# More scan buffers, paid for with weights that are loaded when needed: a bidirectional state-space layer and a soft mixture of experts on one Trainium2 core

## The chip, the cores and the metric

The program runs on one core of one Trainium2 chip. A core has five engines that run side by side, each through its own instructions in a fixed order: TensorE (PE in the profile, its weight loads PEld), VectorE (DVE), ScalarE (ACT), GpSimd (POOL) and SyncE (SP), which here only issues DMA transfers. They wait for each other through semaphores. Working data lie in SBUF (128 partitions), matmul results in PSUM.

The metric is the device time of one execution in microseconds. Before the change its median was 5327.67 us over three runs (5324.82 to 5328.87).

## What is computed

The input is x, 16 sequences of 512 positions with 256 numbers each. The first layer is a state-space layer that runs in both directions, with a residual and a layer norm; the second is a soft mixture of 16 experts with 64 slots each, again with a residual and a layer norm.

```python
xr = x @ in_proj_w.T
xf, res = jnp.split(xr, [D_INNER], axis=-1)              # 512 channels each
xf = silu(causal_dw_conv(xf, conv_w, conv_b))
y = ssm(xf, res, ...)                                    # forward
xb = silu(causal_dw_conv(xf, conv_b_w, conv_b_b))
y = y + ssm(xb, res, ..., reverse=True)                  # backward
x = layernorm(x + y @ out_proj_w.T)

def ssm(x, res, x_proj_w, dt_proj_w, dt_proj_b, A_log, D, reverse=False):
    A = -jnp.exp(A_log)
    delta, B, C = jnp.split(x @ x_proj_w.T, [DT_RANK, DT_RANK + D_STATE], axis=-1)
    delta = softplus(delta @ dt_proj_w.T + dt_proj_b)    # the step sizes, dt
    y = selective_scan(x, delta, A, B, C, D, reverse=reverse)
    return y * silu(res)
...
logits = jnp.einsum('bnd,esd->bnes', layernorm(x), se)
dispatch = softmax(logits, axis=1)
combine = softmax(logits.reshape(b, n, -1), axis=-1)
slots = jnp.einsum('bnd,bnes->besd', layernorm(x), dispatch)
eout = ((gelu(slots @ Wg + bg) * (slots @ Wu + bu)) @ Wd + bd)   # per expert
out = layernorm(x + jnp.einsum('bns,bso->bno', combine, eout))
```

For each of 16 states and 512 channels the selective scan carries a value along the 512 positions: it is multiplied by exp(dt*A) at each step and dt*u*B is added. The result is gated with a factor close to 1 or to 0 (from the reference's small constant in a division), multiplied by C and summed over the states.

## The kernel before

**The scan loop.** `scan_part(b, r, p, ...)` handles batch b, direction r (0 forward, 1 backward) and a pair p of the four 128-channel chunks. It takes the 16 states two at a time, and each pair of states for one chunk is an item: 8 pairs of states x 2 chunks x 2 pairs of chunks x 2 directions x 16 batches are 1024 items. An item goes through the engines like this:

- SP loads B and C of two states, spread over the partitions, into `bs` (L431) and `cs` (L432), three buffers each.
- POOL multiplies du = dt*u by bs into `db` (L442): this is dt*u*B, in three buffers.
- ACT makes the decays exp(dt*A) into a PSUM tile `h` (L459, three buffers) and the gating factor `th` (L461, three).
- VectorE scans, h from decays and db (L465 forward, L467 backward), twice, and writes the gated states `hg` (L470), twice; hg has four buffers.
- POOL multiplies hg by cs in place (L471).
- TensorE adds hg, turned, onto the accumulator `acc` in PSUM (L386), eight pieces of 128 x 128. `add_up(2)` puts an item's add-up behind the work of the two items that follow it. Only then is the item's hg buffer free.

For a few states (four per direction for the first three batches, two later) the product with B goes over TensorE and a matrix with B on its diagonal (`hd`, L420, from `dg` and `duT`); such an item has only half a db tile.

**Side work.** Three queues of generators run beside the items, some pieces after each: `prep` (what the next scan needs), `front` (`finish` and `dispatch` of the batch before) and `back` (experts and combine). `HOLD` in them means that a PSUM bank is held until the next item, `BANKS = 3`. The experts of a pair of batches run beside the odd batches from the third on, the combine of both after them.

- `prep_pair` makes dt for two chunks: a matmul of the step-size weights `dtT` (17 rows, the last one the bias) with `xd` into `pz` (L320), softplus on ACT, a scan for rr on VectorE (L346), and du on POOL (L348). `dtT_f` and `dtT_b` were loaded once, in `steps`.
- `finish` turns the gated sum y over TensorE (`pyt`), copies it out (`yt`, L645), multiplies it by the output weights `outT` (`po`, L651), adds x, normalises, and makes `x2T`, which `dispatch` multiplies by the slots (`pl`, L710). `outT` was loaded once, in `constants`, and halved there by VectorE.
- `weights` makes the combine's softmax per 128 positions; `load_x2` loads a piece of x2T back into `cx2` (L917), which the matmuls `cl` (L933) read. The load of the next piece is issued right after the matmuls of the present one.

**Buffers and order.** A tag's tiles share a number of buffers, `bufs`; a tile that is written into a buffer waits until everything that read the last one is done. The language's scheduler orders each engine's instructions by the program's order, the free buffers and its own idea of their durations; `late` keeps an instruction in the program's order. SP issues in one order: a load that waits for its buffer holds all loads behind it.

The lines that hold the buffer counts and the order of an item's add-up:

```python
p4 = scan_room.enter_context(tc.tile_pool(name="m_scan", bufs=3))
...
db = p4.tile([P, 2, L], F32, tag="db", name=f"db_{q}_{c}")
...
hg = p4.tile([P, 2, L], F32, tag="hg", name=f"hg_{q}_{c}", bufs=4)
...
evict()
...
beside_scan()
...
add_up(2)
```

Of the kernel before, what the change touches and what calls it, by code (L numbers as in the profile page):

```python
# [17 lines left out]
P = 128  # L18
# [37 lines left out]
def seq_layers(tc, ident, neghalf, a, out):  # L56
# [22 lines left out]
    with ExitStack() as ctx:  # L79
# [76 lines left out]
            late(nc.vector.tensor_scalar(w["xT"][:, :, XC:XW], w["xT"][:, :, XC:XW], 0.5, None, ALU.mult))  # L156

        def steps(w, s, m):
            w["dtT"] = const.tile([DTR + 1, DI], F32, name=f"dtT_{s}")
            nc.sync.dma_start(w["dtT"][:DTR, :], a[f"dt_proj{m}T"])  # L160
            nc.sync.dma_start(w["dtT"][DTR : DTR + 1, :], a[f"dt_proj{m}_b"].unsqueeze(0))
            w["A"] = const.tile([P, ND, NS], F32, name=f"A_{s}")
            nc.sync.dma_start(w["A"], a[f"A{m}_log"].rearrange("(c p) n -> p c n", p=P))
            d = channels(a[f"D{m}"], f"D_{s}")
            w["diagD"] = const.tile([P, ND, P], F32, name=f"diagD_{s}")
            for c in range(ND):
                late(nc.vector.tensor_scalar(w["diagD"][:, c, :], ident, d[:, c : c + 1], None, ALU.mult))
# [7 lines left out]
        def constants():  # L175
            blanks(1)
            steps(side[0], "f", "")
            projections(side[1], "b", "_b")
            steps(side[1], "b", "_b")
            outT = const.tile([P, ND, DM], F32, name="outT")  # L180
            nc.sync.dma_start(outT, a["out_projT"].rearrange("(c p) o -> p c o", p=P))
            late(nc.vector.tensor_scalar(outT, outT, 0.5, None, ALU.mult))
            return outT

        projections(side[0], "f", "")
        blank = p2.tile([P, 4 * DM], F32, tag="W", name="blank", bufs=3)
# [125 lines left out]
        def prep_pair(b, r, p, v):  # L312

            w = side[r]
            yield GAP + 2
            pzs = []
            for c in (2 * p, 2 * p + 1):
                q = f"{b}_{r}_{c}"
                pz = bank(f"pz_{q}")
                nc.tensor.matmul(  # L320
                    pz, w["dtT"][:, c * P : (c + 1) * P], v["xd"][: DTR + 1, :], start=True, stop=True
                )
                pzs.append((c, q, pz))
            yield HOLD
            dts = {}
            for c, q, pz in pzs:
                dts[c] = dt = p4.tile([P, L], F32, tag="dt", name=f"dt_{q}", bufs=4)
                if len(dts) == 1:
                    act = nc.scalar.activation(dt, pz, AF.Softplus)
                    late(act)  # L330
                else:
                    with tc.high_priority():
                        nc.scalar.activation(dt, pz, AF.Softplus)
            yield HOLD
            for c, q, pz in pzs:
                dt = dts[c]

                rr = p4.tile([P, L], F32, tag="rr", name=f"rr_{q}", bufs=4)
                if r == 0:
                    edge, o, i = slice(L - 1, L), rr[:, 0 : L - 1][:, ::-1], slice(1, L)  # L340
                    ins = [t[:, i][:, ::-1] for t in (dt, pz)]
                else:
                    edge, o, i = slice(0, 1), rr[:, 1:L], slice(0, L - 1)
                    ins = [t[:, i] for t in (dt, pz)]
                nc.gpsimd.memset(rr[:, edge], 0.0)
                late(nc.vector.tensor_tensor_scan(o, ins[0], ins[1], 0.0, ALU.add, ALU.max))  # L346
                du = p4.tile([P, L], F32, tag="du", name=f"du_{q}", bufs=4)
                nc.gpsimd.tensor_tensor(du, dt, v["u"][:, c, :], ALU.mult)  # L348
                v[c] = [dt, rr, du]
# [57 lines left out]
        def scan_part(b, r, p, v, accs, done, then):  # L407
# [17 lines left out]
            for n in range(0, NS, 2):  # L425
                q = f"{b}_{r}_{p}_{n}"
                k = 1 if n + 1 in ds else 2

                bs = p4.tile([P, 2, L], F32, tag="bs", name=f"bs_{q}")
                cs = p4.tile([P, 2, L], F32, tag="cs", name=f"cs_{q}")  # L430
                nc.sync.dma_start(bs[:, :k, :], v["bc"][0, n : n + k, :].unsqueeze(0).to_broadcast([P, k, L]))  # L431
                nc.sync.dma_start(cs, v["bc"][1, n : n + 2, :].unsqueeze(0).to_broadcast([P, 2, L]))  # L432
                if n + 3 in ds:
                    dg = p4.tile([P, L], F32, tag="dg", name=f"dg_{q}", bufs=1)
                    nc.sync.dma_start(
                        dg.rearrange("p (l s) -> p l s", l=NL),
                        diag_dram[r, ds.index(n + 3), :, : P * P].rearrange("l (p s) -> p l s", p=P),
                    )
                for c in chunks:
                    dt, rr, du = v[c][:3]  # L440
                    db = p4.tile([P, 2, L], F32, tag="db", name=f"db_{q}_{c}")
                    nc.gpsimd.tensor_tensor(  # L442
                        db[:, :k, :], du.unsqueeze(1).to_broadcast([P, k, L]), bs[:, :k, :], ALU.mult
                    )
                    hg = p4.tile([P, 2, L], F32, tag="hg", name=f"hg_{q}_{c}", bufs=4)
                    hs = {}
                    for j in range(2):
                        if j < k:
                            dec = h = ps_h.tile([P, L], F32, tag="h", name=f"h_{q}_{c}_{j}")
                            hs[j] = (h, dec, db[:, j, :])  # L450
                        else:
                            h = made.pop((n + j, c))
                            dec = p4.tile([P, L], F32, tag="dec", name=f"dec_{q}_{c}", bufs=2)
                            hs[j] = (h, dec, h)

                    ths = {}
                    for j in range(2) if k == 2 else (1, 0):
                        s = slice(n + j, n + j + 1)
                        nc.scalar.activation(hs[j][1], dt, AF.Exp, scale=w["A"][:, c, s])  # L459
                        ths[j] = p4.tile([P, L], F32, tag="th", name=f"th_{q}_{c}_{j}")  # L460
                        nc.scalar.activation(ths[j], rr, AF.Tanh, bias=LN_1E12 / 2, scale=w["Ah"][:, c, s])  # L461
                    for j in range(2):
                        (h, dec, add), th = hs[j], ths[j]
                        if r == 0:
                            nc.vector.tensor_tensor_scan(h, dec, add, 0.0, ALU.mult, ALU.add)  # L465
                        else:
                            nc.vector.tensor_tensor_scan(  # L467
                                h[:, ::-1], dec[:, ::-1], add[:, ::-1], 0.0, ALU.mult, ALU.add
                            )
                        nc.vector.scalar_tensor_tensor(hg[:, j, :], th, 1.0, h, ALU.add, ALU.mult)  # L470
                    nc.gpsimd.tensor_tensor(hg, hg, cs, ALU.mult)  # L471
                    pending.append(
                        (r == n == 0, n == 0, r == 1 and n == NS - 2, c, hg, accs, w, v["u"], f"acc_{q}_{c}", done)
                    )
                    evict()

                    nxt_n = n if c == chunks[0] else n + 2
                    if nxt_n + 1 in ds:
                        for x in sides:
                            x.take_up()  # L480
                        by_diagonal(nxt_n + 1, chunks[1] if c == chunks[0] else chunks[0])
                    beside_scan()
                    if k == 1:
                        diags.pop(0)
                    add_up(2)
# [145 lines left out]
        def finish(b, y):  # L631

            xt = load_x(b)
            for h in range(NL // 2):
                yts = []
                for lc in (2 * h, 2 * h + 1):
                    yield 1
                    pt = bank(f"pyt_{b}_{lc}")
                    for c in range(ND):
                        nc.tensor.transpose(  # L640
                            pt[:, c * P : (c + 1) * P], y[:, c, lc * P : (lc + 1) * P], ident
                        )
                    yield HOLD
                    yt = p2.tile([P, L], F32, tag="fr", name=f"yt_{b}_{lc}")
                    late(nc.scalar.copy(yt, pt))  # L645
                    yts.append(yt)
                yield GAP + 1
                po = bank(f"po_{b}_{h}")
# [264 lines left out]
            expert_done.add(g)  # L913

        def load_x2(b, lc):
            t = p2.tile([P, NM, P], F32, tag="cx2", name=f"cx2_{b}_{lc}")
            nc.sync.dma_start(t, x2_dram[b, :, :, lc * P : (lc + 1) * P].rearrange("k p l -> p k l"))  # L917
            return t

# [119 lines left out]
        fwd = {}  # L1039
        prep.add(1, prep_forward(0, 0, ND, fwd))  # L1040
        prep.drain()
        outT = constants()
        prep.add(1, prep_pair(0, 0, 0, fwd))
        prep.drain()
        for w, s in zip(side, "fb"):
# [101 lines left out]
```

## Time and profile before

| what | us |
|---|---|
| median of three runs | 5327.67 |
| the profiled execution, its own time | 5322.25 |
| its span | 5320.5 |
| busy: POOL, VectorE, TensorE, ScalarE | 4681.6, 4560.6, 4310.4, 4104.9 |
| start of the last multiply of a gated state by cs (L471) | 5077.7 |
| L471 on POOL, one (median) | 2.362 |
| L442 on POOL, one of 128 x 1024 (median) | 2.357 |
| a scan (L465, L467) and a gated state (L470), one | 1.219, 0.679 |
| an add-up (L386), one of its eight pieces (median) | 0.273 |

In the profile a group's line gives the engine, the operation, the tile written and those read, the number of instructions, their busy time, the mean of one in ns, and after the second bar the idle time of the engine just before them with what ended most of it. A row of the waits says who waited for whom: the total in us, how often, and the longest. In a row of the timeline the first number is the start, the second the duration, and the square bracket the idle time of the engine before it. The slices cut the span into 40 equal parts of 133 us. Every engine's record can be put beside the item that it belongs to, since each engine's order is known; where a text says that the trace was paired item by item, this is what is meant.

### The profile page before, as it was taken

What the parts mean: (1) busy time and instruction counts of PE and PEld (TensorE: products, weight loads), DVE (VectorE), ACT (ScalarE), POOL (GpSimd) and SP (SyncE); (2) the same over time, 40 slices, a digit from 0 to 9 for tenths busy, and PEclk for the clock granted to TensorE, in tenths of its full rate; (3) what the DMA queues carried; (4) which work ended last, traced back from release to release, by engine and by line L of the source; (5) the groups of instructions that cost most, each with busy time, mean ns of one, the idle gap of its engine ahead of it and who ended that gap; (6) DMA issues with size and microseconds to landing.
All of it is one profiled execution on the core that took longest, in us unless ns stands there. A gap on an engine that the chain in (4) does not pass through costs nothing. (4 is left out here: it accounts for less than half of the span.)

```text
span 5320.5 us, 74550 instructions
## 1 busy us (share of the span) xinstructions
PE 4310.4 (81%) x24498; PEld 3411.1 (64%) x24498; DVE 4560.6 (86%) x6284; ACT 4104.9 (77%) x6573; POOL 4681.6 (88%) x2537
## 2 busy tenths in 40 slices
PE   5677776897778978788788878889787897878889
PEld 3556565676567756676666766667666676657667
DVE  7999999889998899888898888988898889987733
ACT  6777878887888877888887887888778887777644
POOL 6999999989999899999999989998999989988710
PEclk7778888998899989999899988899888998889999
DMA  5444444675446644576446754467544664447545
GB/s 141 137 129 152 126 142 131 211 234 152 146 146 224 222 144 143 171 226 206 132 140 198 236 169 151 134 210 230 157 151 144 217 227 149 144 153 230 168 135 168
DMA packets 614820, 907.82 MB, mean 171 GB/s; under 512 B 84606, under 2 KB 404734, under 8 KB 614432
## 3 DMA queue, kind: packets, MB, share of 16 engines
q1 hardware_dynamic: 532740, 859.35, 50.9%
q10 hardware_dynamic: 81692, 43.70, 3.1%
q8 instruction: 195, 3.19, 0.2%
q14 instruction: 193, 1.58, 0.1%
HBM read 840.34 MB, written 62.56 MB: 170 GB/s over the span
## 5 line engine op out<-in xcount | busy, mean ns | idle before, releaser
L471 POOL TENSOR_TENSOR hg<-hg,cs 128x1024 f32<-128x1024 f32 x1024 | 2416.9, 2364 | 125.0 <-DVE hg L470 108.0
L442 POOL TENSOR_TENSOR db<-du,bs 128x1024 f32<-128x1024 f32 (+1 forms) x1024 | 2087.7, 2042 | 227.8 <-DVE h L465 84.1
L470 DVE SCALAR_TENSOR_TENSOR hg<-th,h 128x512 f32<-128x512 f32 x1744 | 1156.8, 679 | 183.4 <-PE acc L386 105.9
L386 PE MATMUL acc<-ident,hg 128*128 128x128 f32 x8192 | 1163.6, 292 | 106.4 <-POOL hg L471 84.6
L386 PEld LDWEIGHTS acc<-ident,hg 128*128 128x128 f32 x8192 | 1034.4, 152 | 284.6 <-POOL hg L471 131.3
L467 DVE TENSOR_TENSOR_SCAN h<-h,db 128x512 f32<-128x512 f32 x872 | 1044.9, 1219 | 104.9 <-ACT h L459 92.6
L465 DVE TENSOR_TENSOR_SCAN h<-h,db 128x512 f32<-128x512 f32 x872 | 1044.1, 1219 | 44.5 <-ACT h L459 43.6
L461 ACT ACTIVATE th<-rr,Ah_f 128x512 f32<-128x512 f32 x1024 | 724.6, 714 | 200.9 <-DVE hg L470 198.1
L461 ACT ACTIVATE th<-rr,Ah_b 128x512 f32<-128x512 f32 x1024 | 721.3, 712 | 153.5 <-DVE hg L470 143.5
L459 ACT ACTIVATE h<-dt,A_f 128x512 f32<-128x512 f32 x872 | 591.4, 680 | 99.5 <-DVE hg L470 96.3
L459 ACT ACTIVATE h<-dt,A_b 128x512 f32<-128x512 f32 x872 | 592.3, 680 | 85.6 <-DVE hg L470 81.7
L420 PE MATMUL hd<-dg,duT 128*128 128x128 f32 x2432 | 375.7, 305 | 73.2 <-ACT duT L364 27.1
L420 PEld LDWEIGHTS hd<-dg,duT 128*128 128x128 f32 x2432 | 347.9, 220 | 84.5 <-ACT duT L364 29.5
L710 PE MATMUL pl<-x2T,seT 128*128 128x512 f32 x512 | 294.1, 704 | 78.4 <-DVE hg L470 37.4
L838 PE MATMUL peo<-Wd,ht 128*128 128x256 f32 x1024 | 258.1, 408 | 63.2 <-DVE rr L346 36.6
L869 PEld LDWEIGHTS pg<-st,Wg 128*128 128x128 f32 x2048 | 243.1, 195 | 94.1 <-issue 82.8
L811 PE MATMUL pu<-st,Wu 128*128 128x128 f32 x2048 | 255.6, 284 | 49.3 <-DMA Wu<-in_Wu_dram 27.0
L1015 PE MATMUL cpo<-ceo,ct 128*128 128x256 f32 x1024 | 256.0, 407 | 43.2 <-DVE rr L346 40.0
L811 PEld LDWEIGHTS pu<-st,Wu 128*128 128x128 f32 x2048 | 245.9, 199 | 60.6 <-DVE h L467 29.5
L838 PEld LDWEIGHTS peo<-Wd,ht 128*128 128x128 f32 x1024 | 205.5, 206 | 106.1 <-DVE rr L346 39.2
L869 PE MATMUL pg<-st,Wg 128*128 128x128 f32 x2048 | 265.0, 284 | 4.5 <-DMA st<-s_dram 3.4
L1015 PEld LDWEIGHTS cpo<-ceo,ct 128*128 128x128 f32 x1024 | 207.2, 207 | 87.2 <-DVE rr L346 42.7
(165 smaller groups left out, 6754.0 us busy)
## 6 DMA issues: line engine op xcount, KB each, us to landing
cs<-bc SPq DMA_DIRECT2D x512, 512.0 KB, 3.9
bs<-bc SPq DMA_DIRECT2D x360, 512.0 KB, 5.2
Wg<-in_Wg_dram SPq DMA_DIRECT2D x128, 512.0 KB, 5.7
Wu<-in_Wu_dram SPq DMA_DIRECT2D x128, 512.0 KB, 5.8
Wd<-in_Wd_dram SPq DMA_DIRECT2D x128, 512.0 KB, 5.5
dg<-diag_dram SPq DMA_DIRECT2D x152, 256.0 KB, 4.3
bs<-bc SPq DMA_DIRECT2D x152, 256.0 KB, 3.5
x<-in_x_dram SPq DMA_DIRECT2D x32, 512.0 KB, 6.5
```

What stands on the lines that cost most here:

```text
L386: ins = nc.tensor.matmul(accs[c][:, s], hc[:, j, s], ident, is_transpose=True, start=False, stop=(last and j == 1 and lc == NL - 1),)
L420: ins = nc.tensor.matmul(h[:, s], v[c][3][:, s], dg[:, s], start=True, stop=True)
L442: nc.gpsimd.tensor_tensor(db[:, :k, :], du.unsqueeze(1).to_broadcast([P, k, L]), bs[:, :k, :], ALU.mult)
L459: nc.scalar.activation(hs[j][1], dt, AF.Exp, scale=w["A"][:, c, s])
L461: nc.scalar.activation(ths[j], rr, AF.Tanh, bias=LN_1E12 / 2, scale=w["Ah"][:, c, s])
L465: nc.vector.tensor_tensor_scan(h, dec, add, 0.0, ALU.mult, ALU.add)
L467: nc.vector.tensor_tensor_scan(h[:, ::-1], dec[:, ::-1], add[:, ::-1], 0.0, ALU.mult, ALU.add)
L470: nc.vector.scalar_tensor_tensor(hg[:, j, :], th, 1.0, h, ALU.add, ALU.mult)
L471: nc.gpsimd.tensor_tensor(hg, hg, cs, ALU.mult)
L811: nc.tensor.matmul(pu[:, fc * P : (fc + 1) * P], got["Wu", e][:, k, fc * P : (fc + 1) * P], st[:, k, :, j * SL : (j + 1) * SL], start=(k = ...
L838: nc.tensor.matmul(po[:, j * DM : (j + 1) * DM], ht[:, fc, :], got["Wd", e0 + j][:, fc, :], start=(fc == 0), stop=(fc == NF - 1),)
L869: nc.tensor.matmul(pg[:, fc * P : (fc + 1) * P], got["Wg", e][:, k, fc * P : (fc + 1) * P], st[:, k, :, j * SL : (j + 1) * SL], start=(not ...
```

## The change

Two tags get one buffer more: hg five instead of four, db four instead of three. Room is made in three places. The step-size weights are no longer kept; each `prep_pair` loads the 256 columns that it needs, in two pieces, into one buffer. The output weights are no longer kept either; each `finish` loads them into the buffer of x2T, and the factor 0.5 moves from the weights to the copy of the turned y (a scaled activation in place of a copy). And cx2 has one buffer instead of two.

```diff
         def steps(w, s, m):
-            w["dtT"] = const.tile([DTR + 1, DI], F32, name=f"dtT_{s}")
-            nc.sync.dma_start(w["dtT"][:DTR, :], a[f"dt_proj{m}T"])
-            nc.sync.dma_start(w["dtT"][DTR : DTR + 1, :], a[f"dt_proj{m}_b"].unsqueeze(0))
+            w["dtT"] = [(slice(0, DTR), a[f"dt_proj{m}T"]), (slice(DTR, DTR + 1), a[f"dt_proj{m}_b"].unsqueeze(0))]
...
             steps(side[1], "b", "_b")
-            outT = const.tile([P, ND, DM], F32, name="outT")
-            nc.sync.dma_start(outT, a["out_projT"].rearrange("(c p) o -> p c o", p=P))
-            late(nc.vector.tensor_scalar(outT, outT, 0.5, None, ALU.mult))
-            return outT
...
         def prep_pair(b, r, p, v):
             w = side[r]
+            dtT = p1.tile([DTR + 1, 2 * P], F32, tag="dtT", name=f"dtT_{b}_{r}_{p}")
+            for rows, src in w["dtT"]:
+                nc.sync.dma_start(dtT[rows, :], src[:, 2 * p * P : 2 * (p + 1) * P])
             yield GAP + 2
...
-                    pz, w["dtT"][:, c * P : (c + 1) * P], v["xd"][: DTR + 1, :], start=True, stop=True
+                    pz, dtT[:, (c - 2 * p) * P : (c - 2 * p + 1) * P], v["xd"][: DTR + 1, :], start=True, stop=True
...
-                    db = p4.tile([P, 2, L], F32, tag="db", name=f"db_{q}_{c}")
+                    db = p4.tile([P, 2, L], F32, tag="db", name=f"db_{q}_{c}", bufs=4)
...
-                    hg = p4.tile([P, 2, L], F32, tag="hg", name=f"hg_{q}_{c}", bufs=4)
+                    hg = p4.tile([P, 2, L], F32, tag="hg", name=f"hg_{q}_{c}", bufs=5)
...
         def finish(b, y):
             xt = load_x(b)
+            outT = p1.tile([P, ND, DM], F32, tag="x2T", name=f"outT_{b}")
+            nc.sync.dma_start(outT, a["out_projT"].rearrange("(c p) o -> p c o", p=P))
...
-                    late(nc.scalar.copy(yt, pt))
+                    late(nc.scalar.activation(yt, pt, AF.Identity, scale=0.5))
...
         def load_x2(b, lc):
-            t = p2.tile([P, NM, P], F32, tag="cx2", name=f"cx2_{b}_{lc}")
+            t = p2.tile([P, NM, P], F32, tag="cx2", name=f"cx2_{b}_{lc}", bufs=1)
...
-        outT = constants()
+        constants()
```

## The prediction

> **What bounds the kernel now.** I read the busy shares first, then the slices, then the groups of the scan loop, then the waits.
>
> ```profile
> PE 4310.4 (81%) x24498; PEld 3411.1 (64%) x24498; DVE 4560.6 (86%) x6284; ACT 4104.9 (77%) x6573; POOL 4681.6 (88%) x2537
> ...
> POOL 6999999989999899999999989998999989988710
> ...
> L471 POOL TENSOR_TENSOR hg<-hg,cs 128x1024 f32<-128x1024 f32 x1024 | 2416.9, 2364 | 125.0 <-DVE hg L470 108.0
> L442 POOL TENSOR_TENSOR db<-du,bs 128x1024 f32<-128x1024 f32 (+1 forms) x1024 | 2087.7, 2042 | 227.8 <-DVE h L465 84.1
> L470 DVE SCALAR_TENSOR_TENSOR hg<-th,h 128x512 f32<-128x512 f32 x1744 | 1156.8, 679 | 183.4 <-PE acc L386 105.9
> ```
>
> POOL is the fullest engine, at nine tenths or more nearly everywhere until the scans end (last multiply by cs ends at 5080.1 us); the last 240 us hold almost no POOL work. Of 4788 us between 133 and 4921 us it works 4466 (the forty slices of the windows view, its first and last ones left out), so 322 us is the most that any smoother feed can give. An item (one pair of states for one chunk, 1024 of them) costs POOL 2.04 + 2.36 = 4.40 us, while the scans take about 4.9 us an item. The line L470 holds the wait that the fifth buffer is about: VectorE stands 105.9 us before writing a gated state because TensorE has not yet added up the one that held the buffer.
>
> ```profile
> DVE hg L470 <- PE acc L386: 105.9, 89, 4.8
> ...
> DVE h L467 <- POOL db L442: 11.5, 4, 3.2
> ```
>
> These are two rows of the waits of VectorE: total, times, longest. Waiting for dt*u*B costs it 11.5 us in all. One such stall, in the timeline near 2460 us:
>
> ```profile
> 2459.41 1.23 DVE L467 TENSOR_TENSOR_SCAN h<-h,db 128x512 f32<-128x512 f32 x1 [0.18 <-ACT h L459]
> 2463.01 1.28 DVE L470 SCALAR_TENSOR_TENSOR hg<-th,h 128x512 f32<-128x512 f32 x2 [2.37 <-PE acc L386]
> ...
> 2461.93 1.04 PE L386 MATMUL acc<-ident,hg 128*128 128x128 f32 x8
> ...
> 2464.43 2.37 POOL L471 TENSOR_TENSOR hg<-hg,cs 128x1024 f32<-128x1024 f32 x1 [2.61 <-DVE hg L470]
> ```
>
> TensorE did expert matmuls from 2455.96 and came to the add-up at 2461.93; VectorE lost 2.37 us and POOL, right after it, 2.61. So a late TensorE reaches the fullest engine through the four buffers.
>
> **Part 1, fifth hg buffer.** I paired the trace item by item. POOL's multiply of an item ends a median 9.0 us before the add-up of the same item ends (three quarters within 11.7, worst 24.4), but begins only 2.25 us after VectorE finished it. So buffers are held by TensorE's lag, not by POOL's. In the paired records 92 items have such a stall, 107.5 us, and 95.5 of these lie in stalls under 3 us. One buffer more is worth one item, 4.9 us; the two longest stalls are 4.79 and 4.13. So nearly all can go. How much reaches POOL: matching each stall with POOL's idle time for the same item gives 33.5 us, and with the next item's too 66.0. The same-item match misses idle that comes one step later, the other may count idle with another cause; I take the middle, 50 us. Both ends stay for the range, and so does all of it, 107.5.
>
> **Part 2, fourth db buffer.** Alone it gives nothing. In the built order POOL's multiplies by cs stood 4 db products behind (886 of 1024; now 5, 891 of 1024). Before, product i+3 waited for the scan of item i to free one of three buffers and came just ahead of multiply i, which needs item i as well. Now product i+4 waits for that same scan, and comes just ahead of the same multiply. POOL stays tied to the same event of VectorE; VectorE gets one product more in reserve, worth at most the 11.5 us above. I take 0 (bounds 0 and 11.5).
>
> The Trainium skill's "Perfetto Trace Analysis", section Identifying Performance Opportunities (Optimization Strategy), says that repeating gaps on the engine that should be full can mean too few buffers. Read so, POOL's 125.0 + 227.8 us before L471 and L442 would go, leaving about 4975 us; the pairing disagrees, since POOL then waits for the same item one instruction later.
>
> **Part 3, step-size weights.** 64 pairs now load two pieces each (16 and 1 rows of 256 numbers), 128 issues less four at the start. An issue costs SP 0.32 to 0.4 us (the rows of cs and cx), so some 45 us on a queue with 2126 issues that mostly waits. The single buffer makes the load wait for the previous pair's pz (L320). Behind it in SP's new order stand bs and cs loads. Putting the old trace's times of that pz against the release of the last cs ahead of it, SP is held at most 9.9 us in the running stage (43.8 once at the start, where nothing is ahead). But a cs lands at least 10.9 us, median 20.4, before its multiply, and a bs mostly 13 or more; the weights still land over 20 us before pz. The cover is those landings: 0. Were it gone, 64 holds of about 6 us would cost up to 384.
>
> **Part 4, output weights.** 16 loads of 512 KB, each into the buffer of x2T, after the last use of the previous one (L710). By the same pairing that use is at most 1.8 us later than SP's position, and po (L651) needs the tile 45 us or more later, against landings of 3.7 to 6.5 us. 8 MB more beside 908. The 0.5 moves from one VectorE instruction at the start into 64 evictions on ACT: 586 ns as COPY (L645), 680 to 770 as a scaled ACTIVATE (L727: 716; L691: 770): 64 x 0.10 to 0.19 = 6 to 12 us on an engine 77% busy. PE waits for yt in all some 33 us (15.4 + 13.6 + 2.4 + 1.6), so a few of them are on the path; I take 5 of 0 to 12.
>
> **Part 5, one cx buffer.** 60 loads of 128 KB wait for the cl matmuls just ahead (L933) instead of those one block back. The next use comes 7.7 us later at the closest (block 14, in the last 100 us) and mostly 12 to 25 later; landings take 2.5 to 5.4. Once, near 4970 us, SP is held 15.8 us with two cs behind it, less than the 20 us they usually have. I take 0; were all eight late ones 2 us short, 16.
>
> POOL and VectorE will overlap a little more. The multiplies by cs run 2332 to 2418 ns, whatever VectorE does beside them, so I cost that at 0; if every POOL product went from median 2362 to 2418, 2048 of them would add 115 us. The Trainium skill's "GPSIMD Engine Reference", section Key points, speaks against the change here: the two share their SBUF interfaces, and contend when a VectorE instruction has two inputs in SBUF. In the loop VectorE's second input is h in PSUM, and the narrow spread shows no such contention; by the rule the upper bound just named would be the thing to fear.
>
> **Sum.** 50 - 5 = 45 us off a span of 5320.5, so 5275.5. Around it lie 1.75 us (the profiled execution took 5322.25), and the median shown, 5327.67, is 5.4 above that: 5283.
>
> **Rivals.**
>
> *The gain stays off the path (no change).* VectorE also waits for ACT's decays (92.6 + 43.6 us), for th (39.4) and in its side work for TensorE (72.4 for pl, 56.7 for peo). And in the expert slices TensorE is all but full: 123.63 of 133 us between 1064 and 1197. A late add-up there is not jitter; one more buffer is used up once and the stalls return. For: by the pairing 96.8 of the 107.5 us lie in the odd batches from 3 on, where experts run, 9 to 10 in each such slice. Against: they come singly (batch 7, 2161 to 2494 us, has eleven, of 13.6 us together, mostly 20 us and more apart, each shorter than one item), and over that batch TensorE works 289.39 of 333 us. With 5 to 15 us passing and 5 lost: 5327, range 5317 to 5333.
>
> *TensorE is fed later (slower).* The built order puts VectorE's side work up to four instructions, a whole item, further behind the scans: ht by 1.18 places on average, eo 1.17, xf 1.27, x 1.78, nm 0.82, while TensorE's order stays. Summed over the groups (128 of ht, 128 of nm, 64 each of cnm, eo, xf, cx, 32 of x and of its moments) that is some 635 places, at 0.95 us (mean of 1.22 and 0.68) about 600 us of later feeding. It costs if those places aren't made up by VectorE no longer standing still: TensorE waits for the evictions, falls behind, and the add-ups with it, so that the fifth buffer fills too. It decides from where more than 50 of the 600 reach POOL. Following the waits back from the last multiply, TensorE holds 1268 of 5080 us of the chain, a quarter; a sixth of 600 less the 45 gained gives 5327.7 + 100 - 45 = 5383. For: in-order TensorE and three banks. Against: places aren't time; an order that puts a scan first also starts it sooner.
>
> *Everything passes (much faster).* All 107.5 with 0 lost: 5220.
>
> **How the numbers follow.** The forecast has 0.58 with its own range 5262 (66) to 5300 (33 less 5), everything passing 0.07, off the path 0.15, later feeding 0.20. Changes under 0.2%, 10.7 us, can't be told from none here. Faster by more than that: 0.65 (the forecast, everything passing); within: 0.15; slower: 0.20. The range 5225 to 5345 takes in the forecast with nearly all of its upper bound, the no-change case and the mild half of later feeding; what it leaves out is everything passing in full and the heavy half.
>
> **What will show it.** The row of VectorE's hg waiting for acc should fall from 105.9 under 40 us, POOL's idle before L471 and L442 from 353 to about 300, and the last multiply should end near 5035. Waits for db should stay near nothing, SP's holds unseen by POOL (bs and cs never named as releasers). Nearly all of it should come from the odd batches (about 332 us each now, with 29 us of POOL idle; the even ones take 312, with 13) and from the last. Wrong would be: TensorE's waits for ht, eo, rr or nm grown by as much as the acc wait fell, or acc still named for 80 us and more.

## The result, and the profile after

The changed kernel took 5368.91 us (median of four runs, 5361.69 to 5372.8), the kernel before in the same comparison 5327.72 us. The ratio is 1.0077, interval [1.0059, 1.0094]: 41 us slower, where 45 us faster had been forecast. The profiled execution took 5365.79 us, with a span of 5363.6.

First the busy shares and POOL's slices of the changed kernel, then the groups that answer to those of before; the lines of the file have moved by three, so L468, L439 and L467 are the old L471, L442 and L470.

```profile
PE 4329.2 (81%) x24498; PEld 3412.6 (64%) x24498; DVE 4541.6 (85%) x6283; ACT 4111.3 (77%) x6578; POOL 4681.7 (87%) x2537
...
POOL 6999999989999899898999889998999989988710
...
L468 POOL TENSOR_TENSOR hg<-hg,cs 128x1024 f32<-128x1024 f32 x1024 | 2422.6, 2369 | 103.8 <-DVE hg L467 60.1
L439 POOL TENSOR_TENSOR db<-du,bs 128x1024 f32<-128x1024 f32 (+1 forms) x1024 | 2092.5, 2047 | 284.5 <-DVE h L462 146.1
L467 DVE SCALAR_TENSOR_TENSOR hg<-th,h 128x512 f32<-128x512 f32 x1744 | 1155.6, 677 | 161.1 <-PE acc L383 74.2
```

POOL has the same work, 4681.7 us against 4681.6, and the others within 19 us of theirs. What grew is standing still. The wait that the fifth buffer was for fell, from 105.9 to 74.2 us, and POOL's wait for gated states from 108.0 to 60.1. But POOL's wait to write db, for a scan that is still to come, rose, and its idle time before both products went from 352.8 to 388.3 us (103.8 + 284.5). So the question is what held the scans. The waits of the changed kernel, ScalarE's rows first and then VectorE's (total, times, longest):

```profile
ACT x L622 <- POOL m_sh L617: 86.3, 16, 7.7
ACT cx L622 <- POOL c_sh L617: 79.6, 21, 6.3
...
DVE h L464 <- ACT h L456: 113.7, 54, 5.9
DVE hg L467 <- PE acc L383: 74.2, 44, 4.9
DVE cx L1025 <- PE cpo L1016: 73.2, 26, 4.9
```

The same places in the kernel before:

```profile
ACT cx L625 <- POOL c_sh L620: 64.8, 21, 7.0
...
ACT x L625 <- POOL m_sh L620: 42.6, 15, 6.2
...
DVE h L467 <- ACT h L459: 92.6, 95, 3.2
...
DVE cx L1024 <- PE cpo L1015: 31.0, 19, 4.3
```

The row of ACT x doubled. It belongs to the layer norm in `finish`: VectorE makes mean and variance (`m_mv`, L52), POOL four small instructions that end in the shift `m_sh` (L614 to L617), and ScalarE scales x by them (L622). VectorE's wait for decays has fewer and longer pieces: 54 of up to 5.9 us where there were 95 of up to 3.2.

To see where the time lies I paired both traces item by item and took each batch from its first scan to the next one's:

```
us per batch        even, 4 to 14 (mean of 6)    odd, 5 to 13 (mean of 5)
before              306.1                        328.9
change              314.8                        329.8
```

The even batches lost 8.7 us each, 52 in six; the odd ones are nearly as they were, batch 3 gained 4 us and batch 15 gained 10. In each of the six even batches ScalarE stands once before it scales x: 0.45 to 0.87 us before, 6.5 to 7.7 us in the change. One such place, batch 8, in the timeline of the changed kernel:

```profile
2585.54 0.18 DVE L52 BATCH_NORM_AGGREGATE m_mv<-m_st 128x2 f32<-128x6 f32 x1
2585.80 1.34 POOL L439 TENSOR_TENSOR db<-du,bs 128x512 f32<-128x512 f32 x1
2587.03 2.41 POOL L468 TENSOR_TENSOR hg<-hg,cs 128x1024 f32<-128x1024 f32 x1
2589.33 1.32 POOL L439 TENSOR_TENSOR db<-du,bs 128x512 f32<-128x512 f32 x1
2590.56 0.29 POOL L614 TENSOR_SCALAR m_rs<-m_mv 128x4 f32<-128x4 f32 x1
...
2584.01 1.05 ACT L964 COPY ct<-ctp 128x512 f32<-128x512 f32 x2
2592.76 0.60 ACT L622 ACTIVATE x<-x,m_sh,m_rs 128x256 f32<-128x256 f32 x1 [7.70 <-POOL m_sh L617]
2593.26 0.67 ACT L456 ACTIVATE h<-dt,A_b 128x512 f32<-128x512 f32 x1
2593.88 1.05 ACT L361 COPY duT<-pdu 128x512 f32<-128x512 f32 x2
2593.97 1.23 DVE L464 TENSOR_TENSOR_SCAN h<-h,db 128x512 f32<-128x512 f32 x1 [5.88 <-ACT h L456]
2594.50 6.53 PE L1016 MATMUL cpo<-ceo,ct 128*128 128x256 f32 x16 [6.24 <-ACT duT L361]
```

And in the kernel before:

```profile
2572.53 0.18 DVE L52 BATCH_NORM_AGGREGATE m_mv<-m_st 128x2 f32<-128x6 f32 x1
...
2576.28 0.22 POOL L617 TENSOR_SCALAR m_rs<-m_mv 128x4 f32<-128x4 f32 x1
...
2577.39 0.57 ACT L274 ACTIVATE res<-pres 128x512 f32<-128x512 f32 x1
2578.41 2.08 ACT L625 ACTIVATE x<-x,m_sh,m_rs 128x256 f32<-128x256 f32 x4 [0.45 <-POOL m_sh L620]
...
2574.61 3.62 PE L1015 MATMUL cpo<-ceo,ct 128*128 128x256 f32 x16
```

Read it from VectorE on. The statistics are ready at 2585.72, but POOL first does three products and comes to the factors at 2590.56, 4.8 us later (before: 3.6); making them takes 2.1 to 2.2 us in both kernels. ScalarE is in order; it reached the scaling at 2585.06, 0.7 us ahead of the statistics. In the kernel before it came at 2577.96, 5.3 us after them. So of the 7.25 us by which the stand grew, 5.9 are ScalarE's earlier arrival, the same in each of the six even batches, and 1.3 are POOL's. Until 2592.76 the decay for the next scan (L456) and the copy of du for the diagonal matmuls (`duT`, L361) stand behind the scaling. VectorE's scan waits 5.88 us for that decay, TensorE 6.24 us for that copy, and its next 16 matmuls take 6.53 us instead of 3.62.

The built order of the even batches explains why ScalarE meets the factors so early. Counted in items, VectorE's statistics come half an item later than before (in batch 4 beside item 273.0 instead of 272.5), the scaling on ScalarE half an item earlier (274.5 instead of 275.0, counted by its gating factors), and on POOL five products of du stand ahead of the factors beyond the multiplies by cs, instead of three. Nothing of that is in the diff: the scheduler places instructions by the free buffers, and their number changed.

### The profile page after: what moved, and what is told of

It reads as the page before. It is cut to its first block, busy times and chain, and to the rows that moved or that the text cites. A ratio compares the mean times of both kernels' runs of the same rounds, so it can differ in the third digit from the quotient of the medians.

```text
span 5363.6 us, 74655 instructions
## 1 busy us (share of the span) xinstructions
PE 4329.2 (81%) x24498; PEld 3412.6 (64%) x24498; DVE 4541.6 (85%) x6283; ACT 4111.3 (77%) x6578; POOL 4681.7 (87%) x2537
## 5 line engine op out<-in xcount | busy, mean ns | idle before, releaser
L468 POOL TENSOR_TENSOR hg<-hg,cs 128x1024 f32<-128x1024 f32 x1024 | 2422.6, 2369 | 103.8 <-DVE hg L467 60.1
L439 POOL TENSOR_TENSOR db<-du,bs 128x1024 f32<-128x1024 f32 (+1 forms) x1024 | 2092.5, 2047 | 284.5 <-DVE h L462 146.1
L467 DVE SCALAR_TENSOR_TENSOR hg<-th,h 128x512 f32<-128x512 f32 x1744 | 1155.6, 677 | 161.1 <-PE acc L383 74.2
L456 ACT ACTIVATE h<-dt,A_f 128x512 f32<-128x512 f32 x872 | 592.0, 681 | 115.3 <-DVE hg L467 112.0
L456 ACT ACTIVATE h<-dt,A_b 128x512 f32<-128x512 f32 x872 | 591.1, 679 | 69.4 <-DVE hg L467 67.2
L417 PEld LDWEIGHTS hd<-dg,duT 128*128 128x128 f32 x2432 | 337.0, 214 | 102.6 <-ACT duT L361 35.0
L1016 PE MATMUL cpo<-ceo,ct 128*128 128x256 f32 x1024 | 265.1, 418 | 78.1 <-DVE rr L343 38.6
L870 PEld LDWEIGHTS pg<-st,Wg 128*128 128x128 f32 x2048 | 257.8, 205 | 97.5 <-issue 80.1
L870 PE MATMUL pg<-st,Wg 128*128 128x128 f32 x2048 | 281.1, 295 | 5.6 <-DMA st<-s_dram 3.8
## 6 DMA issues: line engine op xcount, KB each, us to landing
dg<-diag_dram SPq DMA_DIRECT2D x152, 256.0 KB
bs<-bc SPq DMA_DIRECT2D x152, 256.0 KB
```

Of the source, the lines that this page charges most:

```text
L417: ins = nc.tensor.matmul(h[:, s], v[c][3][:, s], dg[:, s], start=True, stop=True)
L439: nc.gpsimd.tensor_tensor(db[:, :k, :], du.unsqueeze(1).to_broadcast([P, k, L]), bs[:, :k, :], ALU.mult)
L870: nc.tensor.matmul(pg[:, fc * P : (fc + 1) * P], got["Wg", e][:, k, fc * P : (fc + 1) * P], st[:, k, :, j * SL : (j + 1) * SL], start=(not ...
L1016: nc.tensor.matmul(po[:, :DM], cts[sc // 4][:, sc % 4 * P : (sc % 4 + 1) * P], eos[sc // 4][:, sc % 4, :], start=(sc == 0), stop=(sc == NS ...
```

## The experiments

Eleven kernels were run, one of them twice. Every ratio is to the kernel before, run beside them on the same chip; its medians there were 5327 to 5333 us.

**One part of the change at a time.** First hg five, db back at three:

```diff
-db = p4.tile([P, 2, L], F32, tag="db", name=f"db_{q}_{c}", bufs=4)
+db = p4.tile([P, 2, L], F32, tag="db", name=f"db_{q}_{c}", bufs=3)
```

> The change with db back at three buffers; hg keeps five, the loads stay as the change has them. Theory A (ScalarE stands before the layer norm's scaling, because GpSimd's factors come later while the scaling comes earlier on ScalarE): in the built order of the even batches from 4 on the statistics stay half an item later on VectorE and the scaling half an item earlier on ScalarE, but only one product of dt*u*B more stands ahead of the factors on GpSimd (4 instead of 3, the change has 5). The stand in even batches falls from 7.7 us to 5 or 6, and the time to 5345-5362 us. Theory B (TensorE is fed later throughout, by VectorE's side work behind the scans): the side work is as late as in the change, so 5360-5375. Theory C (the added loads hold SP and through it the scans): 5360-5375.

Measured 5377.95 us, 1.0089 [1.0075, 1.0102]: the whole loss without the fourth product, and above what any of the three theories had given. ScalarE's row is there in full (`ACT x` for `m_sh`: 85.5 us), and the even batches take 313.0 to 315.7 us.

Then db four, hg back at four:

```diff
-hg = p4.tile([P, 2, L], F32, tag="hg", name=f"hg_{q}_{c}", bufs=5)
+hg = p4.tile([P, 2, L], F32, tag="hg", name=f"hg_{q}_{c}", bufs=4)
```

> The change with hg back at four buffers; db keeps four, the loads stay. Theory A: statistics and scaling stand as before the change, one product more is ahead of the factors on GpSimd; the stand in even batches is 1.5 to 3.5 us (0.5 to 0.9 before, 7.7 in the change), six times 2 us, and VectorE's wait for the add-up is back at about 105 us: 5332-5350 us. Theory B: hg's fifth buffer moved the side work, so it is gone: 5322-5335. Theory C: 5360-5375.

Measured 5336.38 us, 1.0011 [1.0002, 1.0020], the wait for `m_sh` 41.1 us as before. VectorE's wait for the add-up is 77.6 us with these four hg buffers, where 105 had been expected and the change with five has 74.2. And with both buffers undone, so that only the loads, the scaled copy and the single cx buffer are left:

> The change with both buffer counts as before (hg four, db three); the weights loaded when needed, one cx2 buffer and the scaled copy of yt stay. Theories A and B: the order of the three compute engines is that of before, so 5325-5338 us and a stand of under 1 us in the even batches. Theory C: 5360-5375.

Measured 5334.98 us, 1.0008 [0.9999, 1.0017], no difference that could be told. The loads, the scaled copy and the cx buffer together cost some 4 us, at most 9 by the interval, and the loss comes with the fifth hg buffer alone. So Theory C falls. Of Theory A the place holds and the count of products doesn't. With hg alone at five, four products of du stand ahead of the factors, ScalarE comes 0.7 us before the statistics and stands 7.2 to 7.7 us in the even batches. With db alone at four, as many stand ahead, ScalarE comes 5.3 us after the statistics, and it stands 0.01 to 1.8 us.

**Moving the scaling.** If the scaling on ScalarE is the place, it should come later. `finish` yields once more ahead of it, and it is tied behind ScalarE's last gating factor, in every batch:

```diff
+        last_th = [None]
...
-                        nc.scalar.activation(ths[j], rr, ...)
+                        last_th[0] = nc.scalar.activation(ths[j], rr, ...)
...
-            scaled(xt, xt, sh, rs)
+            yield WAIT
+            with tc.issue_after(last_th[0].ins):
+                scaled(xt, xt, sh, rs)
```

> The whole change, and in finish the scaling of x is put one item later in the program and queued on ScalarE behind the gating factor of the item traced last: 1.5 items later on ScalarE in all batches. Nothing else is ordered by hand. Theory A: the stand before the scaling (86 us in all, 7.7 in each even batch) falls under 25 us in all; the even batches lose most of their 9 us each, and the time falls by 35 to 55: 5310-5335 us, and less if what the fifth hg buffer gives then shows. Theory B: the side work of VectorE is as late as in the change: 5355-5375. Theory C: 5360-5375.

Measured 5350.69 us, 1.0039 [1.0025, 1.0052]. The row of x waiting for `m_sh` fell to 6.0 us, and the even batches came back to 306.8 to 310.7 us, so their loss goes with the standing. The time is above the 5310 to 5335 us expected. But the odd batches, whose scaling had stood about as long in the change (3.0 to 4.9 us) as in the kernel before (4.0), became longer, 330.4 to 334.9. The edit isn't a pure move of one instruction: what follows in `finish` comes an item later with it. So it was made for the six even batches alone:

```diff
...
-            scaled(xt, xt, sh, rs)
+            if b % 2 == 1 and 3 <= b < nb - 1:
+                yield WAIT
+                with tc.issue_after(last_th[0].ins):
+                    scaled(xt, xt, sh, rs)
+            else:
+                scaled(xt, xt, sh, rs)
```

(b is the batch that is finished; its finish runs in the next one.)

> The whole change with the scheduler's order; the scaling is queued later on ScalarE (behind the gating factor of the item traced last, one item later) only for the six finishes that run in the even batches 4 to 14; the run that did this in all batches brought the even batches from 315 to 307 us, but lengthened odd ones by 2 to 4. Theory A: odd batches as in the change (327 to 331), even ones 306 to 308: 5369 less 6 times 8, 5315-5328 us. Theory B: the even batches' loss has other parts that come back elsewhere: 5335-5350.

Measured 5291.06 us (5288.81 to 5292.15), 0.9931 [0.9919, 0.9944]: 78 us below the change and 36 below the kernel before, more than was expected. The same place in batch 8 of this kernel's timeline:

```profile
2561.36 0.18 DVE L52 BATCH_NORM_AGGREGATE m_mv<-m_st 128x2 f32<-128x6 f32 x1
2563.92 3.62 PE L1022 MATMUL cpo<-ceo,ct 128*128 128x256 f32 x16
2565.24 0.23 POOL L615 TENSOR_SCALAR m_rs<-m_mv 128x4 f32<-128x4 f32 x1
...
2567.38 2.08 ACT L623 ACTIVATE x<-x,m_sh,m_rs 128x256 f32<-128x256 f32 x4
```

ScalarE no longer stands there (up to 1.2 us in the other five), all four scalings run one after the other, and the 16 matmuls take 3.62 us again. POOL comes to the factors 3.7 us behind the statistics in this batch and 4.9 in the other five, as in the change (3.7 to 4.9); what moved is ScalarE, which comes 5.8 to 5.9 us after the statistics instead of 0.7 before.

**Five buffers in the order of four.** The other way to take the reordering out: a dependency that orders, but waits for nothing on the chip, makes the scheduler place a gated state as if four buffers were there, while the tile has five.

```diff
+                added.append(ins.ins)
...
-                        nc.vector.scalar_tensor_tensor(hg[:, j, :], th, 1.0, h, ALU.add, ALU.mult)
+                        gated = nc.vector.scalar_tensor_tensor(hg[:, j, :], th, 1.0, h, ALU.add, ALU.mult)
+                        if len(added) + len(pending) >= 4:
+                            tc.add_manual_dep(gated.ins, added[len(added) + len(pending) - 4].name, ...)
```

(`added` holds the last matmul of each add-up; three points stand for what isn't shown.)

> The whole change (hg five buffers, db four, all loads), but each gated state is ordered behind the add-up of the state four items back as if hg had four buffers; the ordering puts no wait into the program. The built order of TensorE is the same as with four buffers, GpSimd's and ScalarE's differ in few places, statistics and scaling stand where they stood before the change. Theory A1 (the fifth buffer is worth what the prediction said, and only the order that the scheduler makes of it costs): VectorE's wait for the add-up falls under 40 us, the stand before the scaling in even batches is 1.5 to 3.5 us, time 5275-5312 us. Theory A2 (the buffer itself gives nothing, since VectorE then stands for ScalarE's decays or TensorE's side results instead; the order costs): wait for the add-up under 40 us, but 5325-5340 us. Theory D (five buffers cost by themselves, whatever the order): 5355-5375.

Measured 5340.93 us, 1.0024 [1.0014, 1.0035]. The wait for the add-up left the list and the even batches came back (305 to 308 us), yet the odd ones took 332 to 333. VectorE's waits in this kernel:

```profile
DVE h L466 <- ACT h L458: 124.4, 89, 4.6
DVE nm L725 <- PE pl L720: 86.0, 39, 8.7
DVE hd L466 <- PE hd L419: 65.7, 51, 4.4
```

The buffer without its order buys nothing: VectorE stands for the decays, the logits and the diagonal products instead (92.6, 72.4 and 40.6 us in these rows before). The even batches show the cause of the loss from another side: ScalarE comes 5.3 us after the statistics again, and they take what they took before the change. The same with db three:

> As the run before it, with db at three buffers: hg's fifth buffer alone in the order of four. One product fewer stands ahead of the factors on GpSimd. Theory A1: 5275-5315 us, within 8 us of the run with four db buffers. Theory A2: 5322-5338. Theory D: 5355-5380, as hg's fifth buffer alone gave 5378 with the scheduler's order.

Measured 5352.38 us (5343.32 to 5362.93), 1.0049 [1.0036, 1.0061], between what two of the theories had given; the even batches take 306.4 us on average and the odd ones 333.2.

**Whose gain is it?** The version with the later scaling in the even batches beat the kernel before. That could be the buffers' doing or the later scaling's. So the same edit was put into kernels with fewer buffers, beside a repeat. Into the kernel before:

> The kernel before with one edit: in the six even batches from 4 on, ScalarE's scaling of x after the layer norm comes one item later. All buffers are those of before. It asks whose the 36 us are by which the change with later scaling beat the kernel before. In the kernel before ScalarE stood only 0.45 to 0.87 us ahead of the scaling in each of these six batches, 4 us in all. Theory F: the fifth gated state is worth 30 us and more once the scaling doesn't stand; then this kernel, without that buffer, stays at 5320 to 5332. Theory M: the later scaling itself wins, by what stands behind it on ScalarE and TensorE, whatever the buffers; then 5285 to 5302.

Into the change with hg at four:

> The change with hg back at four buffers (db four, weights loaded when needed) and the same later scaling in the six even batches. With hg four and the scaling where the scheduler put it, it was 1.0011 of before. Theory F: without the fifth gated state the later scaling brings nothing, 5322 to 5338. Theory M: 5288 to 5308.

Into the change with db at three:

> The change with db back at three buffers (hg five) and the same later scaling. The fifth gated state without the fourth product was 1.0089 of before with the scaling where the scheduler put it, the change 1.0077. Theory F: the fifth gated state alone carries the gain, so 5288 to 5300, as the version with both. Theory G: the gain needs both buffers, since only the fourth product lets POOL run an item ahead of the factors; then 5310 to 5335. Theory M gives no difference by buffers, 5286 to 5304.

And the version with both buffers again:

> The change with the later scaling in the six even batches once more, beside the three kernels that have fewer buffers, so that all four share one chip. It was 0.9931 [0.9919, 0.9944] of before. Every theory: 0.990 to 0.996, 5280 to 5305; a ratio above 0.998 would mean that the gain was that chip's.

They took 5351.75, 5361.99, 5323.53 and 5299.07 us. Beside the runs without the edit:

```
ratio to before      scaling where the scheduler put it   one item later in the even batches
hg 4, db 3           1.0008 [0.9999, 1.0017] (loads only) 1.0039 [1.0026, 1.0051] (the kernel before)
hg 4, db 4           1.0011 [1.0002, 1.0020]              1.0064 [1.0052, 1.0077]
hg 5, db 3           1.0089 [1.0075, 1.0102]              0.9985 [0.9976, 0.9994]
hg 5, db 4           1.0077 [1.0059, 1.0094] (the change) 0.9944 [0.9931, 0.9956], earlier 0.9931 [0.9919, 0.9944]
```

Theory M falls: with four hg buffers the later scaling costs 21 to 28 us by these ratios. With five it saves 55 to 78. Theory F named the right buffer, but its times held for the last row alone: it had the kernels with four buffers 20 and 24 us lower, and that with hg alone at five 24 us lower. Neither the buffer nor the place of the scaling gains alone; they do only together. Theory G has a part: with the later scaling the fourth product is worth 24 us (5323.53 to 5299.07), with hg at four it is worth nothing. Why the later scaling costs with four buffers isn't settled. In that form of the kernel before, VectorE's wait for the add-up rose to 121.0 us, and the even batches took 309.4 us instead of 306.1; ScalarE comes 7.6 us after the statistics there, and the scaling starts 0.7 to 1.8 us after its factors are made, so it is later than it need be. Whether that is the cost, no run tried.

**Half of it.** The last run made the move in batches 4, 6 and 8 alone, to see whether each place pays for itself or the whole program flips. Against the version with six:

```diff
-            if b % 2 == 1 and 3 <= b < nb - 1:
+            if b in (3, 5, 7):
```

> The change with the scaling one item later in three of the six even batches only: in 4, 6 and 8, not in 10, 12 and 14. Both buffers stay. Theory F (each late factor costs its own batch, and the one that follows is fed late by it): batches 4, 6 and 8 fall from 314 to 316 to 306 to 309 us and the odd ones behind them, 5, 7 and 9, from 327 to 331 to 323 to 327, while 10, 12, 14 and 11, 13 stay as in the change; half of the 70 to 78 us by which moving all six was below the change, so 5328 to 5338, about 1.000 of before. Theory O (the gain is the whole program's, a clock that is granted higher once enough is moved, or one lucky order): the six even batches or the odd ones move together, and the time is near 5300 or near 5365.

Measured 5334.12 us, 1.0001 [0.9992, 1.0010], where half the gain had been put at 5328 to 5338. Batch by batch, in us:

```
batch                    4      5      6      7      8      9      10     11     12     13     14
change                   314.5  327.2  315.6  329.8  315.4  331.0  314.2  329.9  315.2  331.3  314.2
later in 4, 6, 8         306.5  325.8  308.9  323.8  307.8  323.4  315.6  331.1  314.1  329.6  315.4
later in all six         307.8  323.3  308.0  325.3  306.4  323.3  308.0  323.7  307.9  323.2  308.4
```

Two stands of ScalarE in this kernel, in batch 8 with the edit and in batch 10 without:

```profile
2574.33 2.08 ACT L623 ACTIVATE x<-x,m_sh,m_rs 128x256 f32<-128x256 f32 x4 [1.16 <-POOL m_sh L618]
...
3205.46 0.60 ACT L623 ACTIVATE x<-x,m_sh,m_rs 128x256 f32<-128x256 f32 x1 [7.70 <-POOL m_sh L618]
```

The gain stops where the edit stops, so it is local: 7 to 8 us in the batch itself, and 1 to 8 us in the odd one after it. Theory O falls. Why the odd one gains isn't shown.

## Why the prediction was wrong

**The bound** held. POOL stayed the fullest engine, with the same work to a tenth of a microsecond, and the time is lost in its feed.

**Part 1, the fifth hg buffer**, is the step that failed. It priced the buffer at 50 us, as a wait that goes while everything else stays in its place, and the sum has no term for the order that the scheduler makes of five buffers. The runs show another order and another worth of the wait.

The order: with hg at five ScalarE comes to the layer norm's scaling 5.9 us earlier against the statistics. It stands 6.5 to 7.7 us in each of six even batches, which lose 52 us together, and hg's buffer alone makes the whole loss, 1.0089 [1.0075, 1.0102].

The wait: VectorE's wait for the add-up fell to 74.2 us and not under 40. Where it is gone, with five buffers in the order of four, the kernel is 13 us slower than the one before. So neither its total nor POOL's pairing said what the buffer was worth.

With the scaling moved, a gain of 32 to 36 us against 45 is there and mostly where it was placed: the odd batches take 323.8 us instead of 328.9, batch 3 4.2 less, batch 15 about 12 less, while the even ones take 1.6 more each. But the wait is still 82.6 us in that kernel, and the gain needs the fourth db buffer, which had been put at nothing: with hg alone at five it is 7 us (0.9985 [0.9976, 0.9994]). So it is in part luck that this gain comes near the 45.

**Part 2, the fourth db buffer**, took 0, and alone it gives nothing, as foretold: 1.0011 beside 1.0008 without it. Nor does the product more that stands ahead of the layer norm's factors make ScalarE stand; db alone at four leaves the wait for `m_sh` at 41.1 us. But 0 is 24 us short where hg has five buffers and the scaling is moved.

**Parts 3, 4 and 5** held. The loads, the scaled copy and the cx buffer make 1.0008 [0.9999, 1.0017], some 4 us, against 5 us forecast. The scaled copy itself costs 0.5 us in all (64 at 589 ns against 581), not 6 to 12: the rows it was priced from have other operands. Loads of bs are named once as what POOL waits for (3.8 us), where never had been foretold; before it was twice, 4.6 us in all. Those of cs never are. SP's queue had 2208 issues before, not the 2126 counted there, which changes nothing in the sum.

**The rival "TensorE is fed later"** had the sign, a loss by a new order, and nearly the size, 5383. Its mechanism was another: VectorE's side work an item behind the scans, and TensorE short of it. Much of that order is in the version with the later scaling too: POOL's factors stand there behind as many products as in the change, and VectorE's statistics in the even batches are as late. What the rival lacked is the place: not the mean over 635 places, but one instruction per even batch at which an in-order engine meets a result that isn't ready. **"The gain stays off the path"** fits one of the runs, five buffers in the order of four, though that one lies above its range of 5317 to 5333.

**The tests it named**: the add-up's row fell to 74.2 us, not under 40; POOL's idle time rose to 388.3 instead of falling to about 300; the last multiply by cs ends at 5121.6, not near 5035 (5044.6 with the later scaling); VectorE's waits for db rose from 11.5 to 21.9 us. The 332 and 312 us that it gave the odd and even batches before are 328.9 and 306.1 by the pairing used here.

The advice weighed in Part 2 (the Trainium skill, "Perfetto Trace Analysis", section Identifying Performance Opportunities) reads repeating gaps as a possible lack of buffers. By these runs more buffers help only together with a change of order: 0.9931 [0.9919, 0.9944] with the scaling moved, 1.0077 [1.0059, 1.0094] without.

## What to carry to other kernels

Where a scheduler orders the instructions by free buffers, one buffer more is a new program: compare the built orders on every engine, and for each small instruction whose place moves ask who waits for its result and what stands behind the one who waits. A wait row's total didn't say here what removing it is worth; a cost per stage, paired item by item, and an experiment on half of the places said more. And where two edits touch the same order, try them together as well as alone: here the buffers lost 0.8% and the later scaling 0.4% by itself, and both together gained 0.6 to 0.7%.

## What the runs showed of the hardware

TensorE's clock drops after a long stop. In the changed kernel's batch 8 the windows view (start:end, length, busy time of PE, PEld, VectorE, ScalarE and POOL, then the granted clock, the DMA share and GB/s) shows it around the 6.24 us stop:

```profile
2584.00:2594.50 10.50, 3.75 (x32) 3.56 (x32) 4.62 (x13) 2.81 (x7) 10.08 (x13) 0.95 0.46 162
2594.50:2601.00 6.50, 6.50 (x18) 5.22 (x19) 1.87 (x3) 6.46 (x14) 6.50 (x3) 0.56 0.51 155
```

The granted clock is 0.56 in the stretch in which TensorE has work again, and a stop of 6.2 us costs another 2.9 (6.53 against 3.62 us for the same 16 matmuls). The group of these matmuls rose from 256.0 to 265.1 us. That isn't most of the loss: the time at half clock in an even batch (mean of the six) is 71.1 us in the change and 69.7 before. In the version with the later scaling it is 56.5, and in the odd batches 34.6, against 47.1 in the change and 42.2 before; whether a higher clock there is the gain's cause or its effect, the runs don't tell.

The Trainium skill, "TensorE: Matmul & The Clock Gate", Part 1: The HAM clock gate, says that the clock is halved after an idle window of about 3.4 us and comes back after about as long a busy one. The rows above agree for the halving. For the return they give more: a mean of 0.56 over 6.5 us is about 5.7 us at half clock after TensorE had work again. Shorter stops lie in every trace. In that of the kernel before, put beside the changes of the clock, all 31 stops of 4 to 5 us saw a halving before or within 0.7 us of their end, 18 of 31 of 2.5 to 3 us, and none of 93 of 0.5 to 1 us; so in this trace a stop somewhat under 3.4 us was often followed by one too.
